# Attention values and sums of exponentials on four column tiles of 32, with the inverses carried between partitions

## The chip, the cores and the metric

One NeuronCore of a Trainium2 chip runs the whole program. The metric is the device time of one execution in microseconds (us). Names: PE is TensorE (PEld its weight loads), DVE is VectorE, ACT is ScalarE, POOL is GpSimd. An eviction is the reading of a product out of PSUM, where TensorE's matmuls leave their results. The chain that ended last is the work behind the last instruction, followed back through what each step waited for.

## The reference

Two layers over x of shape (64, 256, 512), float32, with a 256 x 256 matrix of zeros and ones as mask and as graph:

```python
# layer 0: attention under the mask, residual, layer norm
q, k, v = (x @ W + b for each of Wq, Wk, Wv)            # 8 heads of 64
scores = q @ k.T / sqrt(64) + (1 - adj) * -1e9
out = softmax(scores) @ v @ Wo + bo
x = layernorm(x + out)
# layer 1: graph product, residual, layer norm
x = layernorm(x + (adj @ x) @ W1 + b1)
```

## The kernel before

It works in windows of two batches. A window has 4 attention units; a unit is one batch and 4 heads, with heads in pairs `a` and in halves of the partitions `s`. In a window run the attention of this pair of batches, the projections of the next pair and the output side of the last pair, interleaved so that TensorE always has work. 32 windows of 4 units make the 128 units of this text.

A unit ends so: the values (exponentials times V) and the sums (a matrix of ones times the summed exponentials) go into one PSUM tile `at`; one step later DVE divides.

```python
def values(p, u):
    ...
    for a in range(2):
        for kc in range(NC):
            for s in range(2):
                h = 2 * a + s
                nc.tensor.matmul(at[s * HD:(s + 1) * HD, 0, a, :], V[p, g][:, kc, b, h * HD:(h + 1) * HD],
                                 e[kc][:, s, a, :], start=kc == 0, stop=kc == NC - 1)
    for s in range(2):
        nc.tensor.matmul(at[s * HD:(s + 1) * HD, 1].rearrange("p a n -> p (a n)"), ones,
                         sm[:, s].rearrange("p a n -> p (a n)"), start=True, stop=True)
    later(1, divided, p, u, at)

def divided(p, u, at):
    ...
    nc.vector.transpose(z, at[:, 1] ...)        # 32x32 blocks, so that one column holds every query's sum
    nc.vector.reciprocal(rz, z1)                # 128 x 16
    nc.vector.transpose(rs, rz ... )            # and back, spread over the partitions
    nc.vector.tensor_tensor(O..., at[:, 0]..., rs..., op=OP.mult)
    ...
```

A projection is made from seven products of half size (a Strassen-Winograd scheme). Products share PSUM banks, and **later products accumulate onto what an earlier one left there**:

```python
SEVEN = [("a11", 0, 0, True), ("a12", 1, 1, True), ("s2", 4, 0, False), ("s3", 5, 1, True),
         ("s1", 3, 0, False), ("a22", 6, 1, False), ("s4", 2, 0, False)]
# (rows, weight block, bank, begins a new accumulation)

def block_product(key, i, rows, w, weight_first):
    name, t, bank, begins = SEVEN[i]
    if begins:
        BANKS[key, bank] = ps_mm.tile([P, 2, HF], F32, name="mm")
    pm = BANKS[key, bank]
    ...
```

The first product (`a11`) is read out of bank 0 as it is, then the third (`s2`) is added into the same bank. ACT makes that read-out for q: two activations with the bias, 256 columns each. The order of instructions on each engine is decided by a scheduler, not by the source alone.

## Time and profile before

| | before |
|---|---|
| time, median of the 3 runs | 2913.33 us (2910.57 to 2914.95) |
| TensorE busy | 2873.9 us, 99% |
| share of the values (L305) and sums (L308) in the last chain | 8% and 4% |
| one unit, first values matmul to the next projection | 1.778 + 0.958 us |

With TensorE at 99% and in 97% of the chain that ended last, only what its stream loses or what makes it wait moves the time. The lines are in the prediction below.

### The profile page before, as it was taken

To read this page: it belongs to the slowest core of one execution; us is meant where nothing else is said; L and a number is where in the kernel's file an instruction comes from. 1 tells how busy PE (TensorE), PEld (TensorE's weight loads), DVE (VectorE), ACT (ScalarE), POOL (GpSimd) and SP (SyncE) were. 2 spreads that over 40 slices of the span, in tenths; PEclk is the share of its full clock that TensorE was granted. 3 is DMA by queue.
4 is the path that set the end of the run, shared out by engine and by line. 5 is a ranking of instruction groups with operands and counts; after the bars stand their busy time and mean duration, and the time that the engine had idled before them with its cause. 6 is when DMAs were issued, how large, how long until landed. Compare 5 with 4: busy or idle time off the path is not lost.

```text
span 2910.7 us, 36278 instructions
## 1 busy us (share of the span) xinstructions
PE 2873.9 (99%) x15126; PEld 2299.8 (79%) x15126; DVE 1927.0 (66%) x3007; ACT 680.2 (23%) x1153; POOL 173.9 (6%) x328
## 2 busy tenths in 40 slices
PE   8999999999999999999999999999999999999997
PEld 7787888788778878887888788878887888788875
DVE  5566676666766667666667666676666766666766
ACT  2222222222222222222222122222222222222210
POOL 0000000000000000000000000000000000000000
PEclk9999999999999999999999999999999999999999
DMA  4000111101111001111011110111100111101000
GB/s 156 15 30 15 44 44 44 44 1 44 44 44 44 11 33 44 44 44 37 8 44 44 44 44 1 44 44 44 44 22 22 44 44 44 44 1 44 30 29 30
DMA packets 60487, 109.07 MB, mean 37 GB/s; under 512 B 5536, under 2 KB 10912, under 8 KB 60320
## 3 DMA queue, kind: packets, MB, share of 16 engines
q1 hardware_dynamic: 58176, 105.92, 10.6%
q8 instruction: 121, 1.98, 0.3%
q10 hardware_dynamic: 2144, 0.79, 0.1%
q14 instruction: 46, 0.38, 0.0%
HBM read 73.14 MB, written 33.55 MB: 37 GB/s over the span
## 4 chain that ended last, share of the span: by engine, by line
PE 97%; DVE 2%; DMA 1%; issue 0%; POOL 0%; ACTq 0%; POOLq 0%; DVEq 0%; SPq 0%
PE mm L205 67%; PE at L276 8%; PE at L305 8%; PE mm L390 8%; PE at L308 4%; PE mm L218 2%; DVE st L343 0%; DVE r L358 0%; DMA wv<-in_L_gnn_Wv_dram 0%; DVE r L334 0%; DMA r<-in_x_dram 0%; DMA rs<-in_adj_dram 0%; DVE e L284 0%; POOL rstd L351 0%; PE mm L156 0%
## 5 line engine op out<-in xcount | busy, mean ns | idle before, releaser
L284 DVE TENSOR_TENSOR e<-e,adjT 128x1024 f32<-128x1024 f32 x256 | 304.7, 1222 | 122.9 <-ACT e L279 122.9
L279 ACT ACTIVATE e<-at 128x1024 f32<-128x1024 f32 x256 | 248.3, 1021 | 242.8 <-PE at L276 240.3
L231 DVE TENSOR_TENSOR r<-r,mm 128x512 f32<-128x512 f32 x192 | 131.6, 685 | 214.5 <-PE mm L205 214.0
L276 PE MATMUL at<-qT,kT 64*128 64x256 f32 x2048 | 256.7, 389 | 1.2 <-ACT e L279 1.2
L244 ACT ACTIVATE kT<-mm,bk 128x256 f32<-128x256 f32 x256 | 107.2, 469 | 624.3 <-PE mm L205 624.3
L305 PE MATMUL at<-e,v 128*64 128x256 f32 x2048 | 249.3, 385 | 0.0
L205 PE MATMUL mm<-wo,o 128*128 128x256 f32 x1024 | 244.9, 382 | 1.8 <-DVE o L173 1.8
L205 PE MATMUL mm<-wv,xT 128*128 128x256 f32 x1024 | 244.2, 382 | 0.0
L390 PE MATMUL mm<-adjT,r 128*128 128x256 f32 x1024 | 237.8, 386 | 6.0 <-issue 4.5
L205 PE MATMUL mm<-w,o 128*128 128x256 f32 x1024 | 242.1, 379 | 0.0
L205 PE MATMUL mm<-xT,wk 128*128 128x256 f32 x1024 | 241.7, 379 | 0.0
L205 PE MATMUL mm<-xT,wq 128*128 128x256 f32 x1024 | 240.2, 382 | 0.0
L256 ACT ACTIVATE v<-mm 128x512 f32<-128x512 f32 x128 | 76.4, 597 | 686.6 <-PE mm L205 686.6
L276 PEld LDWEIGHTS at<-qT,kT 64*128 64x128 f32 x2048 | 187.5, 186 | 61.8 <-issue 43.2
L205 PEld LDWEIGHTS mm<-xT,wq 128*128 128x128 f32 x1024 | 191.9, 190 | 50.3 <-DVE r L358 24.3
L390 PEld LDWEIGHTS mm<-adjT,r 128*128 128x128 f32 x1024 | 194.1, 192 | 42.7 <-issue 15.1
L369 DVE TENSOR_TENSOR r<-r,mm 128x512 f32<-128x512 f32 x256 | 174.6, 682 | 71.4 <-PE mm L205 68.6
L244 ACT ACTIVATE qT<-mm,bq 128x256 f32<-128x256 f32 x256 | 107.4, 471 | 476.2 <-PE mm L205 476.2
L205 PEld LDWEIGHTS mm<-wv,xT 128*128 128x128 f32 x1024 | 195.8, 192 | 27.7 <-issue 0.5
L205 PEld LDWEIGHTS mm<-w,o 128*128 128x128 f32 x1024 | 194.3, 190 | 28.3 <-issue 2.0
L205 PEld LDWEIGHTS mm<-xT,wk 128*128 128x128 f32 x1024 | 194.5, 190 | 27.2 <-issue 0.8
L205 PEld LDWEIGHTS mm<-wo,o 128*128 128x128 f32 x1024 | 191.8, 190 | 30.4 <-issue 3.3
(90 smaller groups left out, 3822.5 us busy)
## 6 DMA issues: line engine op xcount, KB each, us to landing
xc<-in_x_dram SPq DMA_DIRECT2D x128, 256.0 KB, 3.8
r<-in_x_dram SPq DMA_DIRECT2D x32, 1024.0 KB, 5.6
out_dram<-r SPq DMA_DIRECT2D x64, 512.0 KB, 3.5
wv<-in_L_gnn_Wv_dram SPq DMA_DIRECT2D x3, 256.0 KB, 5.6
wq<-in_L_gnn_Wq_dram SPq DMA_DIRECT2D x3, 256.0 KB, 6.0
wk<-in_L_gnn_Wk_dram SPq DMA_DIRECT2D x3, 256.0 KB, 4.5
w<-in_L_gnn_weight_dram SPq DMA_DIRECT2D x3, 256.0 KB, 5.2
wo<-in_L_gnn_Wo_dram SPq DMA_DIRECT2D x3, 256.0 KB, 5.7
```

Source lines behind the costliest of these rows:

```text
L205: nc.tensor.matmul(pm[:, j, :], left[:, k, j * P:(j + 1) * P], right[:, k, :], start=begins and j == 0 and k == 0, stop=k == 1, skip_group ...
L218: nc.tensor.transpose(pt[:, d, :], xs[:, d * P:(d + 1) * P], ident)
L231: nc.vector.tensor_tensor(to, to, pm, op=OP.add)
L244: nc.scalar.activation(to[:, a], pm[:, a], AF.Identity, bias=b[:, 2 * g + a:2 * g + a + 1])
L256: assembled(i, pm, out, lambda to, pm, g: nc.scalar.activation(to, pm, AF.Copy))
L276: nc.tensor.matmul(sc[:, s, a, :], K[p, g][r, kc, a, b, :], Q[p, g][r, :, a, b, :], start=True, stop=True)
L279: nc.scalar.activation(e, sc, AF.Exp, scale=qscale)
L284: nc.vector.tensor_tensor(e, e, adjT[:, kc:kc + 1, :].to_broadcast([P, 4, N]), op=OP.mult)
L305: nc.tensor.matmul(at[s * HD:(s + 1) * HD, 0, a, :], V[p, g][:, kc, b, h * HD:(h + 1) * HD], e[kc][:, s, a, :], start=kc == 0, stop=kc == ...
L308: nc.tensor.matmul(at[s * HD:(s + 1) * HD, 1].rearrange("p a n -> p (a n)"), ones, sm[:, s].rearrange("p a n -> p (a n)"), start=True, sto ...
L369: assembled(i, pm, out, lambda to, pm, half: nc.vector.tensor_tensor(to, to, pm, op=OP.add))
L390: nc.tensor.matmul(pm[:, j, :], R[p][:, b, mc, d * P:(d + 1) * P], adjT[:, mc, :], start=mc == 0, stop=mc == NC - 1)
```

## The change

The intent is to take half of the sums' time from TensorE. Before, each head pair's sum was written on 64 partitions, 64 times the same number, in two matmuls of 512 columns at a time. Now each of the four heads of a unit writes its sum on 32 partitions, and all four run at once over 256 columns. The values go to 32-column tiles too, so that TensorE need not change its tile shape in between. The price: the inverse of a head now lies on only 32 of the 64 partitions that need it, so it is carried to the other 32, by five small ACT copies between DVE's reciprocal and second transpose.

```diff
-                    h = 2 * a + s
-                    nc.tensor.matmul(at[s * HD:(s + 1) * HD, 0, a, :], V[...][:, kc, b, h * HD:(h + 1) * HD], ...)
+                    for r in range(2):
+                        q, h = s * HD + r * 32, (2 * a + s) * HD + r * 32
+                        nc.tensor.matmul(at[q:q + 32, 0, a, :], V[p, g][:, kc, b, h:h + 32], e[kc][:, s, a, :], ...)
         for s in range(2):
-            nc.tensor.matmul(at[s * HD:(s + 1) * HD, 1]..., ones, sm[:, s]..., start=True, stop=True)
+            for a in range(2):
+                q = s * HD + a * 32
+                nc.tensor.matmul(at[q:q + 32, 1, 0, :], ones[:, 0:32], sm[:, s, a, :], start=True, stop=True)
...
-        nc.vector.reciprocal(rz, z1)                       # 128 x 16
+        nc.vector.reciprocal(rz1, z1)                      # 128 x 8
+        rz = small.tile([P, 2, 8], F32, name="rz")
+        nc.scalar.activation(rz, rz1[:, None, :].to_broadcast([P, 2, 8]), AF.Copy)
+        for s in range(2):
+            for a in range(2):
+                here, there = (slice(s * HD + r * 32, s * HD + r * 32 + 32) for r in (a, 1 - a))
+                nc.scalar.activation(rz[there, a], rz1[here], AF.Copy)
...  (second transpose from the carried rz; the guard's sums on 8 columns)
```

More of the change, by code (lines that the diff above doesn't have):

```diff
@@ L303, in values @@
                 for s in range(2):
-                    h = 2 * a + s
-                    nc.tensor.matmul(at[s * HD:(s + 1) * HD, 0, a, :], V[p, g][:, kc, b, h * HD:(h + 1) * HD],
-                                     e[kc][:, s, a, :], start=kc == 0, stop=kc == NC - 1)
+                    for r in range(2):
+                        q, h = s * HD + r * 32, (2 * a + s) * HD + r * 32
+                        nc.tensor.matmul(at[q:q + 32, 0, a, :], V[p, g][:, kc, b, h:h + 32], e[kc][:, s, a, :],
+                                         start=kc == 0, stop=kc == NC - 1)
         for s in range(2):
-            nc.tensor.matmul(at[s * HD:(s + 1) * HD, 1].rearrange("p a n -> p (a n)"), ones,
-                             sm[:, s].rearrange("p a n -> p (a n)"), start=True, stop=True)
+            for a in range(2):
+                q = s * HD + a * 32
+                nc.tensor.matmul(at[q:q + 32, 1, 0, :], ones[:, 0:32], sm[:, s, a, :], start=True, stop=True)
         later(1, divided, p, u, at)
@@ L314, in divided @@
         g, b = UNITS[u]
-        z = one.tile([P, T2], F32, name="z")
-        nc.vector.transpose(z, at[:, 1].rearrange("p a n -> p (a n)"))
+        z = one.tile([P, N], F32, name="z")
+        nc.vector.transpose(z, at[:, 1, 0, :])
         z1 = z.rearrange("p (j k) -> p j k", k=32)[:, :, 0]
-        rz = small.tile([P, 16], F32, name="rz")
-        nc.vector.reciprocal(rz, z1)
+        rz1 = small.tile([P, 8], F32, name="rz1")
+        nc.vector.reciprocal(rz1, z1)
[5 more added lines that the diff above has]
+                nc.scalar.activation(rz[there, a], rz1[here], AF.Copy)
         rs = one.tile([P, T2], F32, name="rs")
-        nc.vector.transpose(rs, rz[:, :, None].to_broadcast([P, 16, 32]))
+        nc.vector.transpose(rs, rz.rearrange("p a j -> p (a j)")[:, :, None].to_broadcast([P, 16, 32]))
         nc.vector.tensor_tensor(O[p, g][:, :, :, b, :].rearrange("p c a i -> p a c i"), at[:, 0].rearrange("p a (c i) -> p a c i", c=NC),
                                 rs.rearrange("p (a c i) -> p a c i", a=2, c=NC), op=OP.mult)
-        seen = small.tile([P, 16], F32, name="seen")
-        nc.gpsimd.tensor_tensor(seen, rz, z1, op=OP.add)
-        nc.gpsimd.tensor_tensor(acc, acc, seen, op=OP.add)
+        seen = small.tile([P, 8], F32, name="seen")
+        nc.gpsimd.tensor_tensor(seen, rz1, z1, op=OP.add)
+        nc.gpsimd.tensor_tensor(acc[:, 0:8], acc[:, 0:8], seen, op=OP.add)
         if u == 3:
```

## The prediction

> **What bounds the kernel now.** I read four views in this order: the page's busy times and the chain that ended last (which engine sets the end), the timeline of the matmul engine around one attention unit (what the touched lines cost there), the records of the `at` tile (what one such instruction takes), and the vector engine's timeline behind a unit (whether the added hop has room). Columns of the groups and timelines: start and length in us, engine, line, operation, names, shapes, count.
>
> ```profile
> PE 2873.9 (99%) x15126; PEld 2299.8 (79%) x15126; DVE 1927.0 (66%) x3007; ACT 680.2 (23%) x1153; POOL 173.9 (6%) x328
> ...
> PE 97%; DVE 2%; DMA 1%; issue 0%; POOL 0%; ACTq 0%; POOLq 0%; DVEq 0%; SPq 0%
> PE mm L205 67%; PE at L276 8%; PE at L305 8%; PE mm L390 8%; PE at L308 4%; PE mm L218 2%; DVE st L343 0%; DVE r L358 0%; DMA wv<-in_L_gnn_Wv_dram 0%; DVE r L334 0%; DMA r<-in_x_dram 0%; DMA rs<-in_adj_dram 0%; DVE e L284 0%; POOL rstd L351 0%; PE mm L156 0%
> ```
>
> TensorE is 99% busy and makes up 97% of the last chain; the granted clock is 0.996. So a nanosecond taken from TensorE's stream is a nanosecond of the kernel, and a nanosecond added on DVE or ACT costs nothing until TensorE waits for it. The change touches L305 (values) and L308 (sums of exponentials): 8% and 4% of the chain. That 12% is the whole field of the gain.
>
> ```profile
> 1022.00 1.95 PE L305 MATMUL at<-e,v 128*64 128x256 f32 x16
> 1023.78 1.03 PE L308 MATMUL at<-sm,ones 128*64 128x512 f32 x4
> 1024.74 0.70 PE L205 MATMUL mm<-wo,ys 128*128 128x256 f32 x2
> ...
> L305 PE MATMUL at<-e,v x2048: 379/379/430, 65.9 to 2852.2; 128*64 128x256 f32 x187
> L308 PE MATMUL at<-sm,ones x512: 592/592/593, 67.7 to 2852.9; 128*64 128x512 f32 x171
> ```
>
> The lengths overlap, so read starts, not durations. One unit (there are 128) takes from 1022.00 to 1024.74: values 1.778 us, sums 0.958 us, the medians over all 128 units. Each fp32 matmul of the source is two instructions (8 in the code, 16 here). In the single records, the instructions of a values group start in pairs, one per column tile of 64: 7 ns apart within a pair, 216 ns from pair to pair. A lone 128-column matmul over 256 columns also comes every 216 ns, so two tiles cost the time of one and the pair is bound by streaming. The first pair takes 267 ns, 51 ns more, for its weight load is exposed. A pair of sums of 512 columns takes 429 ns, twice. Then 93 ns more than the streaming pass before the next 128-column matmul starts: 958 = 429 + 436 + 93. The same 93 ns stands ahead of the values (309 from the last `wv` matmul, less 216). That is the price of a change of tile shape; the values and sums share one shape and pay none between them.
>
> **What the Trainium skill says.** "TensorEngine Tiling (Array Packing)", section Key Properties: changing the tiling mode, not just the tile, drains TensorE, and different tiles run their loads and matmuls in parallel. The trace agrees on both: 93 ns at each change, 7 ns between two tiles. Its Tiling Modes list 128x32 with four tiles; nothing in this trace runs four. "TensorE: Matmul & The Clock Gate", section Measured speedup vs the span model, gives span = one matmul + about 4 ns per further tile and measurements with three column tiles (2.38x) and 16 tiles (10.6x); this trace has 7 ns a tile and only pairs. Same page, section LDWEIGHTS: a load goes with columns, columns/1.2 ns. Here the exposed first load is 104 ns after a change to 128 columns (320 less 216) and 51 ns at 64, so it agrees; at 32 I estimate 26 ns. "ScalarE: Activation LUTs", section What ACT_TABLE_LOAD costs: an activation with immediate scale takes 186 ns + 0.833 ns an element and successive ones overlap by 93 ns. The trace has the 1024-element exp at 1021 ns and the 512-element copy at 597: 0.83 ns an element and 173 ns fixed, which agrees.
>
> **The change on TensorE.** Values: 8 matmuls on two tiles become 16 on four tiles of 32 columns. Every tile still streams 256 columns; there are 32 instructions in 8 groups of four. Time: 8 x 216 + 26 = 1.754 us against 1.778, so -24 ns: the values gain nothing, they are split only so that the sums can be without a change of shape in between. Sums: two matmuls of 512 columns on two tiles become four of 256 on four tiles. Two passes of 216, the last tile up to 14 ns later than before, and the 93 ns drain: 216 + 216 + 14 + 93 = 539 ns against 958, -419 ns, rounded. The unit saves 0.436 to 0.443 us after counting the stagger once or twice; I take 0.436. 128 x 0.436 = 55.8 us, or 1.92% of 2913.3. The QK matmuls (L276), projections and transposes are unchanged, and the order of TensorE's groups is that of before.
>
> Can the sequencer feed it? A unit now has 40 matmuls and 40 loads instead of 20 and 20; a group of four tiles asks 8 instructions per 216 ns, 27 ns each. In steady windows the sequencer passes the semaphore waits of two successive transpose groups (L218), 8 instructions apart, within 125 ns (29 times), so at most 16 ns an instruction. It also runs some 30 to 40 instructions ahead of the array when a unit starts. So issue should not bind.
>
> **The change on DVE, ACT and POOL.**
>
> ```profile
> 1048.10 0.71 DVE L316 STREAM_TRANSPOSE z<-at 128x512 f32<-128x512 f32 x1
> 1048.85 0.25 DVE L319 RECIPROCAL rz<-z 128x16 f32<-128x16 f32 x1
> 1049.13 0.71 DVE L321 STREAM_TRANSPOSE rs<-rz 128x512 f32<-128x512 f32 x1
> 1049.88 0.69 DVE L322 TENSOR_TENSOR o<-at,rs 128x512 f32<-128x512 f32 x1
> ```
>
> Today the four steps follow on one engine without a gap. The first transpose halves: at one element per cycle of 0.96 GHz (the skill's clock for VectorE) 256 elements fewer are 267 ns, so some 0.45 us; the reciprocal of 8 instead of 16 is a few ns less. DVE saves about 128 x 0.27 = 35 us of busy time. Then five copies on ACT: the estimate is 190 ns for the first and about 100 ns of pitch for the others, 0.6 us in a row, or 0.9 us of summed durations (128 x 0.9 = 115 us, ACT to about 795 us, 28%). With two handovers between engines, DVE stands still for about 0.9 us ahead of the second transpose, up to 115 us in all; part of it comes out of time in which DVE waits for TensorE anyway. POOL's sums over 8 instead of 16 columns are nothing.
>
> Does TensorE come to wait? `at` has two buffers; the values' one is wanted again by the second half of the next scores. In the tightest unit that I followed, `o` is done at 1031.6 and that half starts at 1034.4; the chain gets some 0.7 us longer and starts 0.4 us sooner, as does TensorE. The sum of exponentials is ready at 1020.9 for a matmul at 1023.8. The output projection needs the last unit of a window, which ends about 11 us before. All have 2 us or more of slack against 1 us. ACT runs the copies in program order, between evictions; PSUM tiles of products number four, and a product of four matmuls takes 1.73 us, so an eviction 1 us late is absorbed. In the instruction order of the changed kernel DVE sometimes puts another eviction between reciprocal and second transpose, using part of the hop. Only the last unit of the whole run has nothing behind it: +0.7 us once. I allow 1 to 2 us in all for such waits: 2913.3 - 55.8 + 1.5 = 2859.0.
>
> **The rivals.**
> A. Four tiles do not stream at the full rate together. Each fp32 tile reads its own 128 partitions, and two such streams are all that this trace shows at full rate; four double that. If a group took twice 216 ns, values would add 8 x 216 = 1.73 us, the sums would be back at about 0.86 + 0.09: +1.7 us a unit, +218 us, 3130 us. For it speaks only that it is unseen; against it, the pair costs nothing over a single, and the skill lists the mode and measured 16 tiles by its span model.
> B. Issue binds: if a matmul and its load cost 31 ns each (the spacing of the very first instructions after the start, cold), a group takes 252 ns, 10 groups x 36 = 0.36 us a unit of the 0.44 given back: 2903 us. The 125 ns above speak against it.
> C. The hop through ACT makes TensorE wait. If one unit in four (the tightest of each window) stalls by 1 us, 32 us return: about 2891 us. Against it stands the slack of 2 us and TensorE's list of waits today, where no steady wait for DVE or ACT shows.
> D. No drain is shorter than thought, or an extra one comes up between values and sums: 0.09 us x 128 = 12 us, 2870 us. Both now use 32 columns, so I expect none.
>
> **Range and chances.** The arithmetic gives 1.9%, just inside the 2% line (2855.1 us), and it is nearly an upper bound, for every further effect adds time. To be over 2% faster, a unit must save 0.455 us, 0.02 more than I find; I give it 0.12. A and strong forms of B or C together make it slower by over 2% with 0.14, nearly all A. The rest, 0.74, is within 2%. The range of 8 in 10 runs from 2853 (0.47 us a unit) to 2895 (C, or half of B, in full).
>
> **What would show it.** In the changed trace: four values matmuls starting about 7 ns apart and 216 ns from group to group; 1.75 us from the first values to the first sums; 0.54 us from there to the next projection; 93 ns drains unchanged; 17686 matmul instructions; ACT at 28%; DVE idle ahead of its second transpose, released by ACT, near 0.9 us a unit; no new line in TensorE's waits over 2 us in sum. Group spacing over 230 ns proves A or B wrong for me (430 for A, 252 for B), a DVE or ACT releaser of over 10 us in TensorE's waits proves C.

## The result, and the profile after

The changed kernel takes **2891.41 us** (median of 4, 2888.32 to 2893.06), the kernel before 2912.01 (median of 4). The ratio is 0.9927, 95% interval 0.9910 to 0.9944: within 2%, 0.7% faster. (A ratio is the mean time of one kernel's fast runs over that of the other's of the same rounds, so not quite the ratio of the medians.) The time lies in the predicted range, but the gain is 21 us where 54 were forecast (2913.3 to 2859.0), so the forecast of its size failed.

The page of the changed kernel, busy times and last chain:

```profile
PE 2831.1 (98%) x17686; PEld 2278.7 (79%) x17686; DVE 1874.4 (65%) x3007; ACT 812.2 (28%) x1793; POOL 168.5 (6%) x328
...
PE 79%; DVE 11%; DMA 5%; POOL 2%; ACT 2%; issue 1%; SPq 0%; POOLq 0%; ACTq 0%; DVEq 0%
```

TensorE fell from 97% of the chain to 79%: TensorE now waits for others. Yet its own part came out as worked out. The timeline of TensorE around one unit (start, length, engine, line, operation):

```profile
1012.81 1.93 PE L306 MATMUL at<-e,v 128*32 128x256 f32 x32
1014.57 0.61 PE L311 MATMUL at<-sm,ones 128*32 128x256 f32 x8
1015.11 0.70 PE L205 MATMUL mm<-wo,ys 128*128 128x256 f32 x2
```

From start to start the medians over 128 units are 1.751 us for the values and 0.545 for the sums (before: 1.778 and 0.958). In the single records the four tiles start 7 ns apart, and groups follow each other every 216 ns. A unit saves 0.440 us, 128 units 56.3 us. Only 24.2 us of that arrived in the profiled execution (2910.7 to 2886.5). The list of waits shows who took the rest (engine, line, waited for: us in total, times, longest):

```profile
DVE rs L330 <- ACT rz L328: 115.2, 99, 1.2
...
PEld mm L205 <- ACT qT L244: 26.6, 30, 0.9
...
PE mm L205 <- ACT qT L244: 14.5, 30, 0.5
...
PEld mm L205 <- DVE r L378: 11.6, 16, 2.2
```

The 115 us that DVE stands still for the carry is no loss by itself. The new thing is TensorE waiting 30 times, once in nearly every window, for an ACT eviction of q. Here is that place in one window, first in the kernel before (timelines of TensorE, ACT and DVE):

```profile
421.47 3.72 PE L205 MATMUL mm<-xT,wq 128*128 128x256 f32 x16
425.03 1.89 PE L205 MATMUL mm<-xs,wq 128*128 128x256 f32 x8
...
423.51 0.84 ACT L244 ACTIVATE qT<-mm,bq 128x256 f32<-128x256 f32 x2 [4.06 <-PE mm L205]
...
420.68 1.92 DVE L358 TENSOR_SCALAR r<-r,mv,rstd 128x512 f32<-128x512 f32 x4 [1.14 <-POOL rstd L351]
422.51 0.71 DVE L316 STREAM_TRANSPOSE z<-at 128x512 f32<-128x512 f32 x1
```

The first two q products run from 421.47, the third starts at 425.03, 3.56 us later. ACT evicts the first at 423.51 and ends at 424.34, so there are 0.69 us to spare, of which some 0.05 are needed to hand over (see below). Now the same place in the changed kernel:

```profile
417.09 3.72 PE L205 MATMUL mm<-xT,wq 128*128 128x256 f32 x16
421.29 1.99 PE L205 MATMUL mm<-xs,wq 128*128 128x256 f32 x8 [0.48 <-ACT qT L244]
...
419.27 0.22 ACT L324 ACTIVATE rz<-rz 128x16 f32<-128x16 f32 x1 [3.77 <-DVE rz L322]
419.51 0.86 ACT L328 ACTIVATE rz<-rz 32x8 f32<-32x8 f32 x4
420.40 0.84 ACT L244 ACTIVATE qT<-mm,bq 128x256 f32<-128x256 f32 x2
...
418.56 0.44 DVE L319 STREAM_TRANSPOSE z<-at 128x256 f32<-128x256 f32 x1
419.03 0.20 DVE L322 RECIPROCAL rz<-z 128x8 f32<-128x8 f32 x1
```

Read it from the bottom. DVE comes to the sums late, after the normalisation that waits for POOL's roots, and has the reciprocal at 419.23. ACT has the carry ahead of the q eviction in its order, so it waits for DVE and copies until 420.37. The eviction starts 3.31 us after the first q matmul instead of 2.04, and ends at 421.24. The third product needs the same bank and starts at 421.29, 4.20 us after the first instead of 3.56: 0.64 us lost. (The eviction is 1.27 us late, 0.64 us more than the room of 0.69 less the 0.05 from its end to the matmul.) (The 0.48 in brackets counts from the end of the previous matmul, which overlaps the next start by 0.16 in a full stream.) Thirty such stalls sum to 19.4 us.

A second stall is rarer: the third product of the output projection, `wo,ys`, waits for DVE's eviction of the first, in 15 windows, 5.8 us together. DVE in the kernel before, at the same place in another window:

```profile
312.99 1.23 DVE L334 TENSOR_TENSOR r<-r,bo 128x1024 f32<-128x1024 f32 x1 [2.38 <-DMA r<-in_x_dram]
314.13 0.68 DVE L369 TENSOR_TENSOR r<-r,mm 128x512 f32<-128x512 f32 x1
314.73 0.25 DVE L319 RECIPROCAL rz<-z 128x16 f32<-128x16 f32 x1
314.89 1.16 DVE L334 TENSOR_TENSOR r<-r,bo 128x1024 f32<-128x1024 f32 x1
```

and in the changed kernel, with TensorE's waiting matmul:

```profile
310.46 1.23 DVE L343 TENSOR_TENSOR r<-r,bo 128x1024 f32<-128x1024 f32 x1 [3.79 <-DMA r<-in_x_dram]
311.60 0.20 DVE L322 RECIPROCAL rz<-z 128x8 f32<-128x8 f32 x1
311.72 1.18 DVE L343 TENSOR_TENSOR r<-r,bo 128x1024 f32<-128x1024 f32 x1
312.81 0.68 DVE L378 TENSOR_TENSOR r<-r,mm 128x512 f32<-128x512 f32 x1
...
313.55 0.70 PE L205 MATMUL mm<-wo,ys 128*128 128x256 f32 x2 [0.30 <-DVE r L378]
```

The scheduler has moved the eviction (`r<-r,mm`) from between the two bias additions to behind both. The first addition waits for the load of `r`; when that comes late, the eviction is 1.2 us later than it was before, and TensorE waits.

The account of the profiled executions: -56.3 (units) + 19.4 + 5.8 = -31.1 us, against -24.2 measured. A stall costs more than its wait: in the single records the first matmul behind each of these 45 stalls stands 320 ns ahead of the next instead of 216, as behind a change of tile shape, so its weight load is exposed again. At 104 ns each that is 3.1 us behind the q stalls and 1.6 behind the others. In each of 30 windows one other product (`wo,o` behind the transposes) is 0.06 us shorter, -1.8 us; why was not traced. That makes -28.2, and the last 4 us lie in the first and last windows; see experiment e6 for what of them can be had back.

### The profile page after: what moved, and what is told of

Its sections match the earlier page's. It is cut to its first block, busy times and chain, and to the rows that moved or that the text cites. A ratio compares the mean times of both kernels' runs of the same rounds, so it can differ in the third digit from the quotient of the medians.

```text
span 2886.5 us, 41721 instructions
## 1 busy us (share of the span) xinstructions
PE 2831.1 (98%) x17686; PEld 2278.7 (79%) x17686; DVE 1874.4 (65%) x3007; ACT 812.2 (28%) x1793; POOL 168.5 (6%) x328
## 4 chain that ended last, share of the span: by engine, by line
PE 79%; DVE 11%; DMA 5%; POOL 2%; ACT 2%; issue 1%; SPq 0%; POOLq 0%; ACTq 0%; DVEq 0%
PE mm L205 56%; PE mm L399 8%; PE at L276 8%; PE at L306 5%; DVE r L367 3%; DMA r<-in_x_dram 3%; DVE st L352 2%; POOL rstd L360 2%; DMA out_dram<-r 2%; DVE r L378 1%; PE at L311 1%; PE mm L218 1%; DVE r L343 1%; ACT rz L328 1%; DVE ys L173 1%; ACT qT L244 1%
## 5 line engine op out<-in xcount | busy, mean ns | idle before, releaser
L306 PE MATMUL at<-e,v 128*32 128x256 f32 x4096 | 247.7, 382 | 0.0
L324 ACT ACTIVATE rz<-rz 128x16 f32<-128x16 f32 x128 | 27.6, 216 | 748.7 <-DVE rz L322 747.7
L306 PEld LDWEIGHTS at<-e,v 128*32 128x32 f32 x4096 | 119.9, 109 | 108.6 <-issue 41.8
```

The lines of the kernel that those rows point to most:

```text
L306: nc.tensor.matmul(at[q:q + 32, 0, a, :], V[p, g][:, kc, b, h:h + 32], e[kc][:, s, a, :], start=kc == 0, stop=kc == NC - 1)
```

## The experiments

My theory: TensorE's part is as predicted, and the loss is two waits for evictions that an in-order engine makes late: on ACT behind the carry, on DVE behind a bias addition that waits for a load. Rivals: the `at` buffers or the tile shape are at fault; DVE's lateness as such is at fault, whoever carries. Two groups of four kernels, each group on one chip beside the kernel before (medians of nine runs, 2913.89 for e1 to e4 and 2914.41 for e5 to e8). The changed kernel itself ran in neither group, so a time set beside 2891.41 comes from other rounds.

**e1: no carry at all** (half of the inverses go to the wrong head, so the outputs are wrong, relative error 0.08).

```diff
-        rz = small.tile([P, 2, 8], F32, name="rz")
-        ... the five nc.scalar.activation copies
+        rz = rz1[:, None, :].to_broadcast([P, 2, 8])
```

> The inverses are not carried at all, so ACT has no hop (the outputs are wrong on purpose). Theory: TensorE's own part works as predicted (55 us over 128 units) and what is missing is TensorE waiting behind ACT's carry copies: 30 stalls of 0.65 us at the third q product (19.4 us), plus some 6 to 10 us at the output projection's third product and in the tail. Without the carry I expect 2857 to 2866 us and the spacing between the last matmul of the second q product and the first of the third back at 216 ns. Rival (the loss lies in the tile shape or in the attention PSUM buffers, not in the carry): 2885 to 2893 us, as the changed kernel.

Measured: 2867.42 us, ratio 0.9844 (0.9830 to 0.9857). The q stall is gone in all windows: 216 ns there again. It is just over the expected range, for the second stall stays with 6.5 us in 18 windows, although nothing is carried; DVE's order there is that of the changed kernel. So the second stall does not come from the carry.

**e2: ACT's carry queued behind the q eviction** (a window's second unit only).

```diff
+            EVICTED[0] = nc.scalar.activation(to[:, a], pm[:, a], AF.Identity, bias=...)   # in q_or_k
...
+            if u == 1 and EVICTED[0] is not None:
+                order.enter_context(tc.issue_after(EVICTED[0].ins))      # around the five copies
```

> The changed kernel, but ACT's five carry copies of a window's second unit are queued behind the two evictions of the first q product instead of ahead of them; nothing else. Theory: the 30 stalls of 0.65 us go, 19 us, so 2867 to 2875 us. Rival 1 (attention PSUM buffers or the length of the hop as such): no change or slower, 2888 to 2896 us, for the hop gets no shorter.

Measured: 2866.14 us, ratio 0.9837 (0.9824 to 0.9851), correct, just under the expected range. The timelines of TensorE and ACT at the same window:

```profile
415.33 3.72 PE L205 MATMUL mm<-xT,wq 128*128 128x256 f32 x16
418.89 1.89 PE L205 MATMUL mm<-xs,wq 128*128 128x256 f32 x8
...
417.36 0.84 ACT L246 ACTIVATE qT<-mm,bq 128x256 f32<-128x256 f32 x2 [3.62 <-PE mm L205]
418.09 0.21 ACT L329 ACTIVATE rz<-rz 128x16 f32<-128x16 f32 x1
418.34 0.86 ACT L333 ACTIVATE rz<-rz 32x8 f32<-32x8 f32 x4
```

The third product is back at 3.56 us after the first. The same copies, in the same number and on the same engine, cost some 25 us less by medians of different rounds (2891.41 and 2866.14), and 19.8 us less between the profiled executions (2886.5 and 2866.7), for standing behind two instructions instead of ahead of them. In the traces 22.5 us are the q stall with its exposed loads; the second stall, which this edit does not touch, is larger in e2's trace (8.3 us in 17 windows). DVE's idle time for the hop is even longer than in the changed kernel (132.6 us against 115.2), and does no harm. That rules out the length of the hop by itself and the `at` buffers as the cause of the q stall.

**e3: the carry on DVE.**

```diff
-        nc.scalar.activation(rz, rz1[:, None, :]..., AF.Copy)         # and the four of 32 x 8
+        nc.vector.tensor_copy(rz, rz1[:, None, :]...)
```

> The five carry copies run on DVE instead of ACT; ACT's order is that of the kernel before. Theory (order on ACT): the 30 stalls go, 2857 to 2870 us, with DVE some 128 x 5 x 0.1 = 60 us or more busier. Rival 2 (DVE gets through its work too late, whichever engine carries): DVE does more itself, so 2888 us or more.

Measured: 2865.73 us, ratio 0.9838 (0.9825 to 0.9852), correct. No q stall; the second stall is left in 9 windows with 3.6 us. DVE is busy 1985.3 us instead of 1874.4, and most of the other windows take the 87.61 us of e6 below, where nothing is lost: the rival that DVE's work as such is late falls.

**e4: the kernel before plus the hop**, with its 64-column tiles untouched.

```diff
-        nc.vector.reciprocal(rz, z1)
+        nc.vector.reciprocal(rz0, z1)
+        nc.scalar.activation(rz, rz0, AF.Copy)
+        for q in range(4):
+            nc.scalar.activation(rz[q * 32:q * 32 + 32, 0:8], rz0[q * 32:q * 32 + 32, 0:8], AF.Copy)
```

> The kernel before, with its 64-column tiles, plus five ACT copies of the same sizes between reciprocal and second transpose (they copy each value to its own place, so the result stays right). Theory: the same stall at the third q product comes up without any change of tile shape. From the trace of before the first eviction would end about 4.0 us after the first q matmul where the third product is due at 3.56, so about 0.5 us in each of 30 windows: 2924 to 2936 us. Rival (tile shape at fault): 2910 to 2915 us.

Measured: 2933.80 us, ratio 1.0071 (1.0057 to 1.0085), correct: 20 us slower. Its list of waits has the changed kernel's new line, again 30 times, for the q eviction:

```profile
PEld mm L205 <- ACT qT L244: 25.0, 30, 0.9
...
PE mm L205 <- ACT qT L244: 12.9, 30, 0.5
```

The third q product starts 0.59 us late in each of 30 windows, 17.8 us, and the exposed loads behind it take another 3.1. The carry alone makes the main loss, without any change of tile shape. DVE's order in e4 is the old one (eviction between the bias additions), and the second stall is absent.

**e5: the changed kernel with the bias additions later on DVE**, carry left as it is.

```diff
+            ADDED[0] = nc.vector.tensor_tensor(to, to, pm, op=OP.add)     # a later addition of q or k
...
+        with ExitStack() as order:
+            order.enter_context(tc.issue_after(ADDED[0].ins))
+            biased(p, b, bo_s)
```

> The changed kernel (carry on ACT, ahead of the q eviction), but the two additions of the output bias to r are queued on DVE behind a later q addition, so that no eviction of the output projection stands behind a bias addition that waits for the load of r. Theory: the second, rarer stall (third product of the output projection, 5.5 us in the changed kernel's trace, 14 times) goes and the 30 stalls at q stay: 5 to 7 us less than the changed kernel, 2884 to 2887 us. Rival (that stall comes from the carry as well): unchanged, 2889 to 2893 us.

Measured: 2879.92 us, ratio 0.9883 (0.9868 to 0.9898), correct. The second stall is gone and the 30 q stalls stay (19.5 us), as the theory says. The gain was larger than I wrote: 11.5 us between medians of different rounds and 8.0 between the profiled executions (2886.5 to 2878.5), where the changed kernel's trace shows 5.8, or 7.4 with the exposed loads. So the traces agree within 0.6 us, and only the medians differ by more. The changed kernel's trace is of the fastest of its four runs; they spread over 4.7 us and e5's over 1.6. That the slower runs had more of this stall fits, but they have no trace, so it is not shown.

**e6: both remedies, carry on DVE.**

> Carry on DVE and bias additions later: both stalls removed. Theory: 128 units x 0.44 us less what the head and tail lose (some 3 us): 2857 to 2862 us, over 1.7% below before, and better than both kernels. Rival (DVE, with 110 us more work than with the carry on ACT, becomes late elsewhere): 2864 us or more.

Measured: 2857.85 us (2857.30 to 2859.32), ratio 0.9808 (0.9795 to 0.9822), correct. It is the fastest kernel of this study and beats both kernels; its interval lies across the line of 2%. The edit is that of e3 and e5 together. Its busy times and last chain:

```profile
PE 2819.1 (99%) x17686; PEld 2281.5 (80%) x17686; DVE 1985.6 (70%) x3647; ACT 680.3 (24%) x1153; POOL 145.2 (5%) x328
...
PE 98%; DVE 1%; DMA 0%; issue 0%; POOL 0%; ACTq 0%; ACT 0%; POOLq 0%; DVEq 0%
```

TensorE has the chain to itself again. The median window takes 87.609 us against 89.369 before: 1.760 = 4 x 0.440, so a steady window loses nothing at all. The profiled execution is 54.3 us shorter than that of before, 2.0 less than the full 56.3; the first and last windows keep those.

**e7: values back on 64-column tiles**, sums on 32, carry on DVE.

```diff
-                    for r in range(2):
-                        q, h = s * HD + r * 32, (2 * a + s) * HD + r * 32
-                        nc.tensor.matmul(at[q:q + 32, 0, a, :], V[...][:, kc, b, h:h + 32], ...)
+                    h = 2 * a + s
+                    nc.tensor.matmul(at[s * HD:(s + 1) * HD, 0, a, :], V[...][:, kc, b, h * HD:(h + 1) * HD], ...)
```

> Carry on DVE (as e3), sums on four tiles of 32, but the values back on two tiles of 64 columns: a change of tile shape stands between values and sums. Theory: that change costs a drain of 93 ns and an exposed weight load of 26 ns, and the values' first load 25 ns more: 0.14 us a unit, 18 us in all, 2880 to 2887 us. Rival (a change of column tile alone drains nothing): 3 us for the values' load only, 2867 to 2871 us.

Measured: 2876.89 us, ratio 0.9873 (0.9858 to 0.9888), correct. It is 19.0 us slower than e6. It ended below the expected range because I had counted from e3, with its rare stall; in e7 the scheduler left the DVE eviction between the bias additions and the steady windows don't have the stall, so e6 is the right partner. TensorE's timeline:

```profile
1008.91 1.95 PE L305 MATMUL at<-e,v 128*64 128x256 f32 x16
1010.79 0.64 PE L310 MATMUL at<-sm,ones 128*32 128x256 f32 x8
1011.36 0.92 PE L205 MATMUL mm<-wo,ys 128*128 128x256 f32 x3
```

The medians are 1.878 us for the values and 0.569 for the sums, 0.151 us over 1.751 + 0.545; 128 x 0.151 = 19.3 us. The change from 64 to 32 columns drains: 309 ns from the last pair to the sums where 216 would do, 93 ns as at any other change. So splitting the values, which gains only 0.027 us a unit in their own time, is what protects a third of the sums' gain.

**e8: carry on POOL, bias additions later.**

```diff
+        nc.gpsimd.tensor_copy(rz, rz1[:, None, :]...)                 # and the four of 32 x 8; with e5's edits
```

> The carry on POOL, bias additions later. POOL has its own program order, so ACT's evictions are not held: theory 2857 to 2864 us, the same as e6. Against it: POOL's small operations in these traces take 0.2 us and more each and the one for the reciprocal roots 1 us, and DVE waits for the hop; if DVE's lateness counts, 2870 us or more.

Measured: 2859.94 us, ratio 0.9813 (0.9800 to 0.9826), correct. The median window is again 87.609 us, though DVE waits 174.0 us for POOL's copies. It makes no difference to a steady window who carries, as long as no eviction that TensorE waits for stands behind it.

## Why the prediction was wrong

- **What bounds the kernel, and the gain on TensorE: right.** The sum was -0.436 us a unit, measured -0.440. The values' 1.754 us measured 1.751, the sums' 0.539 measured 0.545 (the fourth tile starts 20 ns after the first, 14 were counted), the instruction count 17686 is exact, and the drain ahead of the values stayed (309 ns from the last projection matmul).
- **Rivals A, B and D: rightly set aside.** Four fp32 streams run at the rate of one, 216 ns a group; issue did not bind; the only drains are the old ones. e7 shows the drain that the change avoided.
- **The step that failed: "PSUM tiles of products number four, and a product of four matmuls takes 1.73 us, so an eviction 1 us late is absorbed."** The tiles number four, but a product does not always take a new one: the third goes on in the first one's bank and must wait for its read-out. The room was one product's time less the read-out and the handover ahead of it, 0.69 us in the trace of before, and I had not measured it; the three slacks of 2 us that the prediction does give are of other places. The eviction came 1.27 us late, so TensorE stood 0.64 us and then its weight load 0.10 us, in 30 windows: 22.5 us. I had also read the instruction order of the changed kernel only for DVE; on ACT it showed the carry ahead of the q eviction. e1, e2, e3 and e4 show this cause from four sides.
- **A term mis-sized: the hop.** I estimated 0.6 us for the five copies, with overlaps of 93 ns. They took 1.11 us (419.27 to 420.37): 215 and 207 ns each, with 219 ns from start to start of the small ones. With 0.6 us the eviction would have been 0.8 us late and the stall 0.1 to 0.2, by this trace's spare time; that is an estimate, not a run. It makes 3 to 6 us over 30 windows where 19.4 were measured, so most of the loss needed both: the missing slack and the longer hop.
- **Not foreseen: the order on DVE.** The scheduler moved an eviction behind a bias addition that waits for a load; 5.8 us in the profiled run, 7.4 with the exposed loads. e1, which has it without any carry, and e5, which takes it away, show it. I had even counted the reordering as a help. Why the scheduler moved it is not shown: e7 has the same short transposes and keeps the old place.
- **Rival C was right in kind, its place was wrong and its number luck.** It said one stall of 1 us in a quarter of the units and 2891 us. The count, one unit in four, was right, and the sign set for it came: an ACT releaser of 14.5 us in TensorE's waits, over the 10 named. But it looked to the tightest unit, whose slack I had read at the `at` buffer; the stall is at q, and 0.64 us, not 1, was lost there. That 2891 is also the measured time is luck: the second stall, the exposed loads and the run's ends, none of them in C, made up the difference. The use of "no steady wait for DVE or ACT" as evidence against it was the weak point: that a wait does not show says nothing of how near it is.
- **The load of `r` is open in part.** The traces show what it stands behind: it goes into a tile whose store has to land first (SyncE's queue waits for that store 31 times, 51.4 us), and from its issue to DVE's addition 5.1 to 7.3 us pass in the changed kernel, 5.3 to 7.7 before. The pages' medians from its issue to its landing are 5.5 to 5.6 us in the three kernels with values on 64 columns (before, e4, e7) and 6.0 to 6.6 in the seven with values on 32; why is not shown.

## What to carry to other kernels

When a change puts a small instruction of an in-order engine between two others, ask not only how long it is but what stands behind it in that engine's order, and measure the spare time of the most urgent of these. An accumulation that goes on in a bank which another engine reads in between has, as here, less than the time of one product for that read-out (0.69 us of room), however many PSUM tiles there are. And compare the instruction order on every engine before and after: a reordering by the scheduler is part of the change.

## What the Trainium skill lacked or had wrong

- "TensorEngine Tiling (Array Packing)" says that a change of mode drains TensorE, without a size. Here it is 93 ns at each change, also from 128x64 to 128x32 (e7), and then the first weight load stands exposed: 104 ns at 128 columns, 51 at 64, 24 at 32 (first group of sums in e7, 240 ns against 216).
- "TensorE: Matmul & The Clock Gate" has no measurement of four column tiles over all 128 rows, nor of fp32. Here four fp32 tiles of 32 columns over 256 columns take 216 ns a group, the same as one matmul of 128 columns, with 7 ns between tiles where the page has about 4.
- "ScalarE: Activation LUTs" has successive activations overlap by 93 ns. The copies of 32 x 8 elements did not overlap: 207 ns each and 219 ns from start to start. The two evictions of 256 columns behind them do, by 0.10 us (0.47 long, 0.37 from start to start).
- No page of it has a measured time for a PSUM bank that is read between two accumulations into it: here the next matmul starts 0.05 us after the read-out ends (421.24 to 421.29).
